# A decoder layer on one core: gate and latent projections as one 144-column matmul, with the latent transposed afterwards

## The chip, the core and the metric

The kernel runs on one core of a Trainium2 chip. The metric is the device time of one execution in microseconds, as the median of several timed runs. Besides these there is one profiled execution, whose trace gives a record for each instruction of each engine: TensorE (PE) for matmuls, with its weight loads listed apart (PEld), VectorE (DVE), ScalarE (ACT), GpSimd (POOL) and SyncE (SP), which issues most of the DMAs. All data are fp32.

## The reference

One decoder layer for 4 batches of 512 tokens with 512 channels. It has three parts, each followed by a residual addition and a layer norm:

- differential causal attention: 8 heads, each from two score maps with a softmax each; their difference weighted by a scalar lambda; a root-mean-square norm of each head's output, and an output projection
- a selective state-space scan over a context input: convolution of 4 taps, projections to step size, B and C, and for 512 channels x 16 states a recurrence over 512 positions; the result is gated by silu of the attention part's output
- a mixture of experts, which is where the change is made. For the tokens x2 of a batch (512 x 512):

```
xl     = x2 @ Wdown.T                        # latent, 512 x 128
probas = sigmoid(x2 @ Wg.T)                  # 16 experts, 512 x 16
w      = the 8 largest of probas + biases keep probas, scaled to a sum of 2.5
acc    = sum_e w[:, e] * ((xl @ rw1[e].T * sqrelu(xl @ rwg[e].T)) @ rw2[e].T)
out    = shared(x2) + acc @ Wup.T
```

Here sqrelu is the squared relu, and shared is a gated unit of the same kind on x2.

## The kernel before

Tokens are tiled by 128 partitions: a batch has four token tiles. Attention runs over 16 units, each a group of two heads and one batch (function attention). The scan (function scan) takes for each batch 16 states x 2 halves of the channels, so 128 steps, each with a product, a recurrence and a second product on DVE, two exponentials on ACT, and an accumulating DMA to a scratch array by POOL. The experts (function experts) run per batch: the scan's result is gated, transposed and added (pt_y), normalized, and the normalized tokens are transposed into x2T (pt_x): four tiles of 128 channels x 512 tokens. From x2T come the routing scores, the latent and the shared part; then follow 16 experts of two halves each (pg, ph, pa), and the output (ps_y).

The routing scores are made with the tokens as weights: for each token tile and each of the four channel tiles, a matmul of 16 columns (w_g), into one PSUM tile ps_gate. Tokens are then on partitions, as the choice of the eight largest needs them: sigmoid on ACT into pr; sc, m8, rp, sp and pr on DVE; then four transposes pt_w, the copy wT, and a DMA to a scratch array, from which each expert's weights are spread over the partitions (wb). The latent is made the other way round, with w_d as weights and x2T as the data: four matmuls of 512 columns into ps_lat, which ACT copies to xl with the latent channels on partitions. That is the layout in which the experts multiply it, as data of pg and, times wb, as data of ph (tile xw).

Nothing is issued in the order of the text. All operations are recorded first with a key, the time at which they are due: nc.key, set by each part of the kernel, plus an offset from the table SHIFT, found by the name of the written tile and the first letter of its engine ("ps_gate.t" is the matmul into ps_gate). The function order then goes through the recorded operations with a fixed table of durations, takes on each engine the ready one with the smallest key, watches how many buffers of a tag are free, and so fixes the order on every engine before the program is built. For this reason all lines of the trace are line 352, where the operations are issued, and groups are told apart by tile names.

Buffers are counted by tag. PSUM: "mm" has three banks (projections, scan inputs, ps_gate, ps_lat, ph, ps_y), "s" three, "tr" one (all transposes), "po" one. In SBUF the tag "c2" has seven slots of 512 columns and holds w_in, w_dt, xm, xd, w_d, yb (batch 0), wb, xw and ht; w_d stays in its slot to the end. w_g takes the slot of w_xp. "pT" has two slots, and w_d and w_g are loaded by one DMA each, on SP's queue, at the key t_unit(15) - 10.

Of the kernel before, what the change touches and what calls it, by code (L numbers as in the profile page):

```python
# [13 lines left out]
AF = mybir.ActivationFunctionType  # L14
# [5 lines left out]
P = 128  # L20
ENGINES = ("tensor", "vector", "scalar", "gpsimd", "sync")

SHIFT = {
    "aT.s": 14, "a_neg.s": 8, "a_neg.v": -9, "bc.s": 7, "bq.s": -2, "cw.s": -2, "da.g": -4, "da.s": -1, "db.s": 3,
    "dt.v": -12, "du.v": 20, "e.s": 8, "e.v": -1, "gb.s": -1, "h.v": -4, "ht.v": -6, "kT.s": 4, "ln_mv.v": -13,
    "ln_nb.v": -7, "ln_rs.g": -2, "ln_st.v": 9, "ln_ve.v": 1, "lo.v": 9, "ls.v": -5, "lt.s": 6, "m.v": -4, "ms.v":
    -4, "nlam.v": -11, "o.s": -17, "obb.s": 9, "pT.s": -3, "pa.t": 1, "pg.t": -4, "pg_s.t": -8, "ph.t": 3,
    "ph_s.t": 3, "po.t": -10, "pr.s": -8, "pr.v": -20, "ps_gate.t": -17, "ps_in.t": -2, "ps_out.t": 5, "ps_v.t":
    1, "ps_x.t": 11, "ps_y.t": -3, "pt_o.t": 3, "pt_w.t": -8, "pt_x.t": 4, "pt_y.t": -12, "relu.s": 23,
    "relu_s.s": -4, "res.g": -4, "res.s": 7, "res.v": -2, "rp.v": -16, "rs.g": 6, "rs.v": -12, "sc.v": -2, "sg.s":  # L30
    -5, "sg.v": 4, "sgc.s": 5, "sh.v": 6, "sp.v": 14, "sq.s": 4, "sub.v": -9, "v.v": 2, "w.s": 7, "wT.s": -1,
    "w_d.s": 4, "w_dt.s": 9, "w_e.s": 24, "w_g.s": 4, "w_in.s": -31, "w_u.s": 1, "w_xp.s": 3, "x2T.s": -13,
    "xd.s": 9, "xl.s": 3, "xm.g": 2, "xm.s": 1, "xw.v": 2, "y.g": -5, "y.s": 6, "y.v": -5, "yb.s": 6, "yb.v": 5,
}
B, S, HID = 4, 512, 512
NT = S // P
# [3 lines left out]
CTX, DI, NST, DTR, KC = 256, 512, 16, 16, 4  # L40
ND = DI // P
LAT, FH, NE, SCALE = 128, 256, 16, 2.5
NEG = -1e30

# [319 lines left out]
def decoder_kernel(  # L366
# [11 lines left out]
    sb = Pool(ctx.enter_context(tc.tile_pool(name="sb", bufs=1)))  # L378
    ps = Pool(ctx.enter_context(tc.tile_pool(name="ps", bufs=1, space=PSUM)), psum=True)
    dram = Pool(ctx.enter_context(tc.tile_pool(name="scratch", bufs=1, space=DRAM)))  # L380

    ident = fixed.tile([P, P], F32, tag="ident", name="ident")
# [10 lines left out]
    nc = Notes(real)  # L393

    def load(shape, src, tag, name=None, bufs=1, most=0):
        t = sb.tile(shape, tag, name or tag, bufs, most)
        nc.sync.dma_start(out=t, in_=src)
        return t

    def small(shape, tag, bufs=8):  # L400
        return sb.tile(shape, tag, tag, bufs)
# [48 lines left out]
    bq = load([P, 32], bqkv, "bq")  # L450
    cw = load([P, ND, KC], convw, "cw")
    cb = load([P, ND], convb, "cb")
    w_in, cT0 = [], sb.tile([P, 2, S], "h", "cT", 5)
    for c in range(2):
        w_in.append(load([P, DI], inT[c * P : (c + 1) * P, :], "c2", "w_in", 7))
        nc.sync.dma_start(out=cT0[:, c, :], in_=ctxT[0, c * P : (c + 1) * P, :])
    xT0 = sb.tile([P, 4, S], "t8", "xT")
    wk0 = load_k(0)
# [4 lines left out]
    w_xp = load([P, ND, 48], xpT.rearrange("(c p) n -> p c n", p=P), "w_xp")  # L463
    lt = load([P, 2, 2, HD], lam4.partition_broadcast(P).rearrange("p (a c d) -> p a c d", a=2, c=2), "qT", "lt", 2)
    sub = load([P, 2], subln, "sub")
    w_dt = load([DTR, DI], dtT, "c2", "w_dt", 7)
    db = load([P, ND], dtb, "db")
    dsk = load([P, ND], dskip, "dsk")
    a_neg = load([P, ND, NST], alog, "a_neg")
# [4 lines left out]
    lp = sb.tile([P, 2, HD], "o", "lp", 2)  # L474
    ls = sb.tile([P, 2], "ls")
    nlam = sb.tile([P, 1], "nlam")
# [8 lines left out]
    res = [sb.tile([P, NT, HID], f"res{b}") for b in range(B)]  # L485
    obb = load([P, HID], ob.partition_broadcast(P), "oT", "obb", 2)
# [10 lines left out]
    y_d = [dram.tile([P, ND, S], f"y{b}") for b in range(B)]  # L497
# [143 lines left out]
    def scan(b):  # L641
# [3 lines left out]
        cT = cT0 if b == 0 else load_cT(b)  # L645
        nc.key = t_scan(b) - (CONV + (AHEAD if b == B - 1 else 0.0)) if b else 0.0
        y = [sb.tile([P, 2, S], "h", "y", 5) for _ in range(2)]
        for d in range(ND):
            pi = ps.tile([P, S], "mm", "ps_in", 3)
            for c in range(2):  # L650
                nc.tensor.matmul(
                    pi, lhsT=w_in[c][:, d * P : (d + 1) * P], rhs=cT[:, c, :], start=(c == 0), stop=(c == 1)
                )
            xm = sb.tile([P, S + KC - 1], "c2", "xm", 7, 2)
            nc.gpsimd.memset(xm[:, : KC - 1], 0.0)
            nc.scalar.copy(xm[:, KC - 1 :], pi)
            cv = y[d // 2][:, d % 2, :]
            nc.scalar.activation(cv, xm[:, :S], AF.Identity, bias=cb[:, d : d + 1], scale=cw[:, d, 0:1])
            for k in range(1, KC):
                nc.vector.scalar_tensor_tensor(cv, xm[:, k : k + S], cw[:, d, k : k + 1], cv, ALU.mult, ALU.add)  # L660
        px = ps.tile([P, S], "mm", "ps_x", 3)
        for k in range(2):
            sg = sb.tile([P, 2, S], "h", "sgc", 5)
            nc.scalar.activation(sg, y[k], AF.Sigmoid)
            nc.vector.tensor_tensor(y[k], y[k], sg, ALU.mult)
        for d in range(ND):
            nc.tensor.matmul(
                px[:48, :], lhsT=w_xp[:, d, :], rhs=y[d // 2][:, d % 2, :], start=(d == 0), stop=(d == ND - 1)
            )
        xd = sb.tile([48, S], "c2", "xd", 7)  # L670
        nc.scalar.copy(xd, px[:48, :])
        nc.sync.dma_start(out=bc_d[b].rows(), in_=xd[DTR:48, :])

# [3 lines left out]
        for k in range(2):  # L677
            dt = sb.tile([P, 2, S], f"dt{k}", "dt")
            du = sb.tile([P, 2, S], f"du{k}", "du")
            lo = sb.tile([P, 2, S], "h", "lo", 5)  # L680
            for j in range(2):
                d = 2 * k + j
# [11 lines left out]
            for j in range(2):  # L694
                d = 2 * k + j
# [4 lines left out]
        for n in range(NST):  # L700
            nc.key = t_scan(b, n) - 15.0
            bc = sb.tile([P, 2, S], "pair", "bc", 2)
            nc.sync.dma_start(out=bc, in_=bc_d[b].state(n))
            for k in range(2):
                nc.key = t_scan(b, n + 0.5 * k)
                h = sb.tile([P, 2, S], "h", "h", 5)
                nc.vector.tensor_tensor(h, dus[k], bc[:, 0:1, :].spread([P, 2, S]), ALU.mult)
                da = das[turn % 2]
                turn += 1
                for j, first in ((0, 0), (1, 1)):  # L710
                    d = 2 * k + j
# [9 lines left out]


    nc.key = t_unit(NG * B - 1) - 10.0
    w_g = load([P, 4, NE], wgT.rearrange("(c p) n -> p c n", p=P), "w_xp", "w_g")
    gb = load([P, NE], gbias.partition_broadcast(P), "gb")
    w_d = load([P, 4, LAT], wdT.rearrange("(c p) n -> p c n", p=P), "c2", "w_d", 7, 1)
    w_s = sb.tile([P, 2, 4, FH], "t8", "w_s")
    nc.sync.dma_start(out=w_s[:, 0, :, :], in_=swgT.rearrange("(c p) n -> p c n", p=P))
    nc.sync.dma_start(out=w_s[:, 1, :, :], in_=sw1T.rearrange("(c p) n -> p c n", p=P))
# [1 line left out]
    w_u = load([P, HID], wuT, "wq", "w_u", 2)  # L731
# [6 lines left out]
    def experts(b):  # L738
        T = t_expert(b)
        nc.key = T - LEAD[b]  # L740
        if b:
            yb = [load([P, 2, S], y_d[b][:, k : k + 2, :], "o", "yb", 2) for k in (0, 2)]
            yb = [yb[d // 2][:, d % 2, :] for d in range(ND)]
        else:
            yb = [load([P, S], y_d[b][:, d, :], "c2", "yb", 7, 4) for d in range(ND)]
        nc.key = max(T - LEAD[b] + 10.0, nc.key + 5.0)
        for i in range(NT):
            sg = sb.tile([P, HID], "pT", "sg", 2)
# [16 lines left out]


        nc.key += 10.0
        pl = ps.tile([P, S], "mm", "ps_gate", 3)
        for i in range(NT):
            for c in range(4):  # L770
                nc.tensor.matmul(
                    pl[:, i * NE : (i + 1) * NE], lhsT=x2T[c][:, i * P : (i + 1) * P], rhs=w_g[:, c, :],
                    start=(c == 0), stop=(c == 3),
                )
        pr = small([P, NT, NE], "pr", 1)
        nc.scalar.activation(pr.flat(), pl[:, : NT * NE], AF.Sigmoid)
        sc = small([P, NT, NE], "sc", 1)
        nc.vector.tensor_tensor(sc, pr, gb.repeat(1, [P, NT, NE]), ALU.add)
        m8 = small([P, NT, 8], "m8", 1)
# [17 lines left out]
        nc.sync.dma_start(out=w_dr[b], in_=wT)  # L797


        pa = ps.tile([P, S], "mm", "ps_lat", 3)  # L800
        for c in range(4):
            nc.tensor.matmul(pa, lhsT=w_d[:, c, :], rhs=x2T[c], start=(c == 0), stop=(c == 3))
        xl = sb.tile([P, S], "kT", "xl", 2)
        nc.scalar.copy(xl, pa)
        nc.key += 5.0
        sh = sb.tile([P, 2, S], "v", "sh", 2)
        for k in range(2):
# [14 lines left out]
        for e in range(NE):  # L822
            nc.key = t_expert(b, e) - WEIGHTS
            w_e = sb.tile([P, 3, FH], "w_e", "w_e", 4)
            nc.sync.dma_start(out=w_e[:, 0, :], in_=rwgT[:, e, :])
            nc.sync.dma_start(out=w_e[:, 1, :], in_=rw1T[:, e, :])
            nc.sync.dma_start(out=w_e[:, 2, :].split(2), in_=rw2T[:, e, :, :])
            wb = sb.tile([P, S], "c2", "wb", 7, 2)
            nc.sync.dma_start(out=wb, in_=w_dr[b].row(e))
            nc.key = t_expert(b, e) - SCALED  # L830
            xw = sb.tile([P, S], "c2", "xw", 7, 2)
            nc.vector.tensor_tensor(xw, xl, wb, ALU.mult)
            for k in range(2):
                nc.key = t_expert(b, e + 0.5 * k)
                pg = ps.tile([P, S], "s", "pg", 3)
                nc.tensor.matmul(pg, lhsT=w_e[:, 0, k * P : (k + 1) * P], rhs=xl, start=True, stop=True)
                ph = ps.tile([P, S], "mm", "ph", 3)
                nc.tensor.matmul(ph, lhsT=w_e[:, 1, k * P : (k + 1) * P], rhs=xw, start=True, stop=True)
                ht = sb.tile([P, S], "c2", "ht", 7, 2)
                glu(pg, ph, ht, sb.tile([P, S], "e", "relu", 3, 2))  # L840
                nc.key += DOWN
                nc.tensor.matmul(
                    pa, lhsT=w_e[:, 2, k * LAT : (k + 1) * LAT], rhs=ht,
                    start=(e == 0 and k == 0), stop=(e == NE - 1 and k == 1),
                )
# [84 lines left out]
```

## Time and profile before

| | |
|---|---|
| timed runs, median of 3 | 1563.35 us (1561.77 to 1566.78) |
| the profiled execution's own time | 1571.12 us |
| its span, first to last instruction | 1569.4 us |
| mean granted TensorE clock | 0.991 |
| PE busy | 1548.7 us, 99% |
| DVE, ACT, POOL busy | 1197.0, 956.5, 196.3 us |
| DMA | 196.18 MB, mean 125 GB/s |

A line of a group reads: line, engine, operation, written tile <- read tiles, shape, count | busy us, mean ns of one | idle time of the engine just before them, and what ended it. A line of the timeline reads: start, length, engine, operation, tiles, number of instructions merged. A line of the stretches gives, for a stretch of time, its length and the busy time of PE, PEld, DVE, ACT and POOL with counts, then the granted PE clock, the DMA engines' busy share and GB/s. Each fp32 matmul makes two records on PE (and two weight loads), a transpose one. The length of a matmul in the trace includes its latency, and the next may start before it ends.

### The profile page before, as it was taken

What the parts mean: (1) busy time and instruction counts of PE and PEld (TensorE: products, weight loads), DVE (VectorE), ACT (ScalarE), POOL (GpSimd) and SP (SyncE); (2) the same over time, 40 slices, a digit from 0 to 9 for tenths busy, and PEclk for the clock granted to TensorE, in tenths of its full rate; (3) what the DMA queues carried; (4) which work ended last, traced back from release to release, by engine and by line L of the source; (5) the groups of instructions that cost most, each with busy time, mean ns of one, the idle gap of its engine ahead of it and who ended that gap; (6) DMA issues with size and microseconds to landing.
All of it is one profiled execution on the core that took longest, in us unless ns stands there. A gap on an engine that the chain in (4) does not pass through costs nothing.

```text
span 1569.4 us, 15790 instructions
## 1 busy us (share of the span) xinstructions
PE 1548.7 (99%) x4944; PEld 851.2 (54%) x4944; DVE 1197.0 (76%) x2036; ACT 956.5 (61%) x2088; POOL 196.3 (13%) x208
## 2 busy tenths in 40 slices
PE   8999999999999999999999999999999999999998
PEld 3566565655656655565665656655445445445443
DVE  6569889687998888898998899898999852542433
ACT  3676566576766557676566668776955553444343
POOL 4101111011111120111111111111111100000000
PEclk9999999998999999999999999999999999999999
DMA  7135576434467663647665566644857741432341
GB/s 264 55 81 108 126 175 141 100 76 99 98 131 190 111 156 61 132 98 152 161 124 126 94 117 155 154 103 101 219 143 151 199 126 54 149 121 76 97 124 51
DMA packets 105523, 196.18 MB, mean 125 GB/s; under 512 B 10896, under 2 KB 45712, under 8 KB 105440
## 3 DMA queue, kind: packets, MB, share of 16 engines
q1 hardware_dynamic: 87008, 128.06, 28.5%
q0 software_dynamic: 18432, 67.12, 25.2%
q8 instruction: 39, 0.64, 0.2%
q14 instruction: 44, 0.36, 0.1%
HBM read 119.25 MB, written 75.89 MB: 124 GB/s over the span
## 4 chain that ended last, share of the span: by engine, by line
PE 96%; DVE 2%; DMA 1%; ACT 1%; issue 1%; SPq 0%; POOLq 0%; DVEq 0%
PE ps_qk L352 21%; PE ps_out L352 14%; PE s L352 9%; PE po L352 9%; PE ps_v L352 7%; PE pa L352 7%; PE pg L352 6%; PE ph L352 6%; PE ps_y L352 3%; PE pt L352 2%; PE pg_s L352 2%; PE ps_in L352 2%; PE ph_s L352 2%; PE pt_o L352 2%; PE ps_dt L352 1%; PE ps_lat L352 1%
## 5 line engine op out<-in xcount | busy, mean ns | idle before, releaser
L352 DVE TENSOR_TENSOR_SCAN h<-da,h 128x1024 f32<-128x1024 f32 x128 | 292.7, 2287 | 2.8
L352 PE MATMUL ps_qk<-xT,wq 128*128 128x512 f32 x512 | 240.5, 593 | 0.0
L352 PE MATMUL ps_out<-ow,oT 128*128 128x512 f32 x512 | 237.6, 595 | 0.0
L352 POOL DMA_DIRECT2D y<-h x128 | 111.3, 869 | 838.2 <-DVE h L352 659.9
L352 ACT ACTIVATE da<-dt,a_neg 128x512 f32<-128x512 f32 (+1 forms) x256 | 174.8, 715 | 45.3 <-DVE h L352 43.6
L352 DVE TENSOR_TENSOR ht<-relu,ph 128x512 f32<-128x512 f32 x128 | 87.2, 684 | 128.8 <-PE ph L352 108.8
L352 PE MATMUL s<-kT,qT 128*128 128x384 f32 (+3 forms) x512 | 170.2, 442 | 0.7 <-DVE nm L352 0.6
L352 PE MATMUL po<-v,pT 128*128 128x256 f32 x640 | 162.1, 384 | 0.4 <-ACT pT L352 0.4
L352 DVE TENSOR_TENSOR h<-h,bc 128x1024 f32<-128x1024 f32 x128 | 156.1, 1219 | 0.9
L352 PEld LDWEIGHTS po<-v,pT 128*128 128x128 f32 x640 | 122.2, 192 | 63.4 <-issue 35.0
L352 DVE TENSOR_TENSOR h<-du,bc 128x1024 f32<-128x1024 f32 x128 | 155.9, 1218 | 0.1
L352 ACT ACTIVATE relu<-pg 128x512 f32<-128x512 f32 x128 | 75.6, 591 | 130.3 <-PE pg L352 116.1
L352 ACT ACTIVATE e<-e,nm 128x128 f32<-128x128 f32 (+3 forms) x256 | 141.8, 556 | 21.6 <-DVE nm L352 20.8
L352 DVE CUSTOM_DVE_ANT_0 e<-s,mask 128x128 f32<-128x128 f32 (+3 forms) x256 | 118.7, 485 | 45.6 <-PE s L352 42.9
L352 PEld LDWEIGHTS ps_out<-ow,oT 128*128 128x128 f32 x512 | 93.3, 191 | 83.1 <-issue 79.8
L352 PEld LDWEIGHTS ps_qk<-xT,wq 128*128 128x128 f32 x512 | 91.9, 190 | 77.3 <-issue 71.9
L352 PE MATMUL pa<-ht,w_e 128*128 128x512 f32 x256 | 131.3, 595 | 1.5 <-DVE ht L352 1.3
L352 PE MATMUL ph<-xw,w_e 128*128 128x512 f32 x256 | 130.3, 592 | 0.0
L352 PE MATMUL pg<-xl,w_e 128*128 128x512 f32 x256 | 129.4, 593 | 0.1
L352 PEld LDWEIGHTS s<-kT,qT 128*128 128x128 f32 x512 | 90.2, 193 | 62.8 <-issue 47.6
L352 PE MATMUL ps_qk<-xT,wk 128*128 128x512 f32 x256 | 120.5, 593 | 0.0
L352 ACT COPY pT<-pt 128x128 f32<-128x128 f32 (+3 forms) x128 | 54.2, 423 | 107.6 <-PE pt L352 106.1
(120 smaller groups left out, 2095.0 us busy)
## 6 DMA issues: line engine op xcount, KB each, us to landing
y<-h POOLq DMA_DIRECT2D x128, 512.0 KB, 7.5
bc<-bc SPq DMA_DIRECT2D x64, 512.0 KB, 6.4
wb<-w SPq DMA_DIRECT2D x64, 256.0 KB, 3.4
xT<-in_xT_dram SPq DMA_DIRECT2D x15, 1024.0 KB, 8.0
w_e<-in_rwgT_dram SPq DMA_DIRECT2D x64, 128.0 KB, 2.2
w_e<-in_rw1T_dram SPq DMA_DIRECT2D x64, 128.0 KB, 2.3
w_e<-in_rw2T_dram SPq DMA_DIRECT2D x64, 128.0 KB, 2.5
wq<-in_wqkvT_dram SPq DMA_DIRECT2D x8, 512.0 KB, 7.2
```

Source lines behind the costliest of these rows:

```text
L352: getattr(getattr(self.nc, s.engine), s.name)(*[get(a) for a in s.args], **{k: get(v) for k, v in s.kw.items()})
```

## The change

The weights w_g (16 columns) and w_d (128 columns) are put side by side in one tile w_dg of 144 columns, with a buffer of its own, filled by two DMAs. For each token tile and channel tile there is one matmul, with the tokens as weights and the 144 columns as data. Two token tiles share a PSUM bank, so ps_gate now consists of two "mm" tiles of 2 x 256 columns, of which 2 x 144 are used. ACT takes the sigmoid of the last 16 columns from each tile, and copies the first 128 columns of each to xr, the latent with tokens on partitions. Four transposes into pt_l (tag "tr") and a copy give xl as before. The matmuls into ps_lat, and w_d and w_g, are gone. The count of "c2" slots becomes C2 = 6, and the whole table SHIFT has new values, so the order of all engines is made anew.

```diff
 SHIFT = {
-    "aT.s": 14, "a_neg.s": 8, "a_neg.v": -9, "bc.s": 7, "bq.s": -2, "cw.s": -2, "da.g": -4, "da.s": -1, "db.s": 3,
...
+    "aT.s": 15.4, "a_neg.s": 12.1, "a_neg.v": -7.8, "bc.s": 7.4, "bq.s": -3.3, "bvb.s": -2.6, "cT.s": -3.5,
...
+    3.2, "po.t": -7.2, "pr.s": -9.5, "pr.v": -13, "ps_dt.t": -0.1, "ps_gate.t": -18.9, "ps_in.t": -1.8,
...
 }
+C2 = 6
...
-        w_in.append(load([P, DI], inT[c * P : (c + 1) * P, :], "c2", "w_in", 7))
+        w_in.append(load([P, DI], inT[c * P : (c + 1) * P, :], "c2", "w_in", C2))
...
-    w_g = load([P, 4, NE], wgT.rearrange("(c p) n -> p c n", p=P), "w_xp", "w_g")
+    w_dg = sb.tile([P, 4, LAT + NE], "w_dg")
+    nc.sync.dma_start(out=w_dg[:, :, :LAT], in_=wdT.rearrange("(c p) n -> p c n", p=P))
+    nc.sync.dma_start(out=w_dg[:, :, LAT:], in_=wgT.rearrange("(c p) n -> p c n", p=P))
     gb = load([P, NE], gbias.partition_broadcast(P), "gb")
-    w_d = load([P, 4, LAT], wdT.rearrange("(c p) n -> p c n", p=P), "c2", "w_d", 7, 1)
...
-        pl = ps.tile([P, S], "mm", "ps_gate", 3)
+        pls, xr = [], sb.tile([P, NT, LAT], "pT", "xr", 2)
+        for k in range(2):
+            pl = ps.tile([P, 2, 256], "mm", "ps_gate", 3)
+            for i in range(2):
+                t = 2 * k + i
+                for c in range(4):
+                    nc.tensor.matmul(
+                        pl[:, i, : LAT + NE], lhsT=x2T[c][:, t * P : (t + 1) * P], rhs=w_dg[:, c, :],
+                        start=(c == 0), stop=(c == 3),
+                    )
+            pls.append(pl)
+        pr = small([P, NT, NE], "pr", 1)
+        for k in range(2):
+            nc.scalar.activation(pr[:, 2 * k : 2 * k + 2, :], pls[k][:, :, LAT : LAT + NE], AF.Sigmoid)
+        for k in range(2):
+            nc.scalar.copy(xr[:, 2 * k : 2 * k + 2, :], pls[k][:, :, :LAT])
+        pt = ps.tile([P, S], "tr", "pt_l", 1)
         for i in range(NT):
-            for c in range(4):
-                nc.tensor.matmul(
-                    pl[:, i * NE : (i + 1) * NE], lhsT=x2T[c][:, i * P : (i + 1) * P], rhs=w_g[:, c, :],
-                    start=(c == 0), stop=(c == 3),
-                )
-        pr = small([P, NT, NE], "pr", 1)
-        nc.scalar.activation(pr.flat(), pl[:, : NT * NE], AF.Sigmoid)
+            nc.tensor.transpose(pt[:, i * P : (i + 1) * P], xr[:, i, :], ident)
+        xl = sb.tile([P, S], "kT", "xl", 2)
+        nc.scalar.copy(xl, pt)
...
-        pa = ps.tile([P, S], "mm", "ps_lat", 3)
-        for c in range(4):
-            nc.tensor.matmul(pa, lhsT=w_d[:, c, :], rhs=x2T[c], start=(c == 0), stop=(c == 3))
-        xl = sb.tile([P, S], "kT", "xl", 2)
-        nc.scalar.copy(xl, pa)
```

More of the change, by code (lines that the diff above doesn't have):

```diff
@@ L23 @@
 SHIFT = {
-    "aT.s": 14, "a_neg.s": 8, "a_neg.v": -9, "bc.s": 7, "bq.s": -2, "cw.s": -2, "da.g": -4, "da.s": -1, "db.s": 3,
[L25 to L33, printed above, removed]
+    "aT.s": 15.4, "a_neg.s": 12.1, "a_neg.v": -7.8, "bc.s": 7.4, "bq.s": -3.3, "bvb.s": -2.6, "cT.s": -3.5,
@@ new lines @@
+    "cf.v": -1.7, "cw.s": -2.2, "da.g": -4.8, "da.s": -1, "db.s": 4.2, "dsk.s": 2.1, "dt.s": -2.1, "dt.v": -7.7,
+    "du.v": 21.2, "e.s": 7.6, "e.v": -2.1, "gb.s": -1.2, "h.v": -4.3, "ht.v": -6.5, "kT.s": 3.9, "l.v": 2.1,
+    "ln_mv.v": -14.5, "ln_nb.v": -33.8, "ln_rs.g": -2.5, "ln_st.v": 4.7, "ln_ve.v": -21.4, "lo.v": 12.6, "lp.v":
+    2.2, "ls.s": -1.8, "ls.v": -6.6, "lt.s": 3, "m.v": -3.7, "ms.v": -4.3, "nlam.v": -8.1, "o.s": -12.8, "oT.s":
+    0.7, "obb.s": 17, "ow.s": -1.2, "pT.s": -2.7, "pa.t": 1, "pg.t": -2.1, "pg_s.t": -8.4, "ph.t": 2.8, "ph_s.t":
@@ new lines @@
+    3.2, "po.t": -7.2, "pr.s": -9.5, "pr.v": -13, "ps_dt.t": -0.1, "ps_gate.t": -18.9, "ps_in.t": -1.8,
+    "ps_out.t": 5.1, "ps_qk.t": 1.3, "ps_v.t": 2.1, "ps_x.t": 12.8, "ps_y.t": 2.9, "pt.t": -0.3, "pt_o.t": 2.7,
+    "pt_w.t": -7.1, "pt_x.t": 1.5, "pt_y.t": -5.9, "qT.s": 0.6, "relu.s": 20.5, "relu_s.s": -3.8, "res.g": -0.4,
+    "res.s": -5.4, "res.v": -1.8, "rp.v": -16.4, "rs.g": 6.5, "rs.v": -12.2, "s.t": 0.9, "sc.v": 4, "sg.s": -1.5,
+    "sg.v": 4.3, "sgc.s": 3.9, "sh.v": 7.5, "sp.v": 15.5, "sq.s": -16.2, "sub.s": -33.5, "sub.v": -9.9, "v.v":
@@ L34 @@
+    1.5, "w.s": 6.4, "wT.s": -1.1, "w_dg.s": 0.9, "w_dt.s": 6.5, "w_e.s": 23.5, "w_in.s": -30.8, "w_s.s": -0.3,
+    "w_u.s": -4.7, "w_xp.s": 1.8, "wb.s": 10.2, "wq.s": 2.4, "wv.s": 5.9, "x2T.s": -13.1, "xd.s": 17.9, "xl.s":
+    2.9, "xm.g": 1.7, "xm.s": 7.8, "xr.s": -1, "xw.v": 3.9, "y.g": -4.6, "y.s": 7.9, "y.v": -9.9, "yb.s": 5.6,
+    "yb.v": 2.7,
 }
@@ L465, in decoder_kernel @@
     sub = load([P, 2], subln, "sub")
-    w_dt = load([DTR, DI], dtT, "c2", "w_dt", 7)
+    w_dt = load([DTR, DI], dtT, "c2", "w_dt", C2)
     db = load([P, ND], dtb, "db")
@@ L653, in scan @@
                 )
-            xm = sb.tile([P, S + KC - 1], "c2", "xm", 7, 2)
+            xm = sb.tile([P, S + KC - 1], "c2", "xm", C2, 2)
             nc.gpsimd.memset(xm[:, : KC - 1], 0.0)
@@ L669, in scan @@
             )
-        xd = sb.tile([48, S], "c2", "xd", 7)
+        xd = sb.tile([48, S], "c2", "xd", C2)
         nc.scalar.copy(xd, px[:48, :])
@@ L744, in experts @@
         else:
-            yb = [load([P, S], y_d[b][:, d, :], "c2", "yb", 7, 4) for d in range(ND)]
+            yb = [load([P, S], y_d[b][:, d, :], "c2", "yb", C2, 4) for d in range(ND)]
         nc.key = max(T - LEAD[b] + 10.0, nc.key + 5.0)
@@ L827, in experts @@
             nc.sync.dma_start(out=w_e[:, 2, :].split(2), in_=rw2T[:, e, :, :])
-            wb = sb.tile([P, S], "c2", "wb", 7, 2)
+            wb = sb.tile([P, S], "c2", "wb", C2, 2)
             nc.sync.dma_start(out=wb, in_=w_dr[b].row(e))
             nc.key = t_expert(b, e) - SCALED
-            xw = sb.tile([P, S], "c2", "xw", 7, 2)
+            xw = sb.tile([P, S], "c2", "xw", C2, 2)
             nc.vector.tensor_tensor(xw, xl, wb, ALU.mult)
@@ L838, in experts @@
                 nc.tensor.matmul(ph, lhsT=w_e[:, 1, k * P : (k + 1) * P], rhs=xw, start=True, stop=True)
-                ht = sb.tile([P, S], "c2", "ht", 7, 2)
+                ht = sb.tile([P, S], "c2", "ht", C2, 2)
                 glu(pg, ph, ht, sb.tile([P, S], "e", "relu", 3, 2))
```

## The prediction, made before the result was known

> **What bounds the kernel now.** I read four views in this order: the page's busy times, the list of what TensorE (PE) waited for, the groups by tile shape, and the timeline of PE around the edited code. The page first.
>
> ```profile
> span 1569.4 us, 15790 instructions
> PE 1548.7 (99%) x4944; PEld 851.2 (54%) x4944; DVE 1197.0 (76%) x2036; ACT 956.5 (61%) x2088; POOL 196.3 (13%) x208
> ```
>
> PE is busy for 1548.7 of 1569.4 us. The 20.7 us that remain are 6.3 at the start, about 7 after its last matmul (it ends at 1562.4) and about 7 of waits in between; the longest waits are these.
>
> ```profile
> PE ps_in L352 <- DMA cT<-in_ctxT_dram: 6.3, 1, 6.3
> PE pt_y L352 <- DVE res L352: 2.4, 3, 0.9
> PE pa L352 <- DVE ht L352: 1.3, 2, 0.8
> ```
>
> (Columns: total us, times, longest.) So what PE has to issue is the time, and an edit is worth what it takes off PE, unless it makes PE wait. The two groups that go, and the transposes that resemble the added ones:
>
> ```profile
> L352 PE MATMUL ps_gate<-w_g,x2T 128*128 128x16 f32 x128 | 15.4, 253 | 0.0
> L352 PE MATMUL ps_lat<-x2T,w_d 128*128 128x512 f32 x32 | 14.5, 592 | 0.0
> L352 PE MATMUL pt_x<-ident,res 128*128 128x128 f32 x64 | 10.3, 279 | 0.2 <-ACT oT L352 0.2
> ```
>
> Each fp32 matmul of the program appears twice here (64 gate matmuls, x128), a transpose once. The means of 253 to 592 ns are latencies that overlap; what counts is the pitch, the distance between starts in a run. It comes from the timeline (start, length, instructions in the run):
>
> ```profile
> 34.43 7.07 PE L352 MATMUL ps_v<-wv,xT 128*128 128x256 f32 x32
> ...
> 41.33 0.61 PE L352 MATMUL s<-kT,qT 128*128 128x128 f32 x4
> ...
> 1049.35 0.60 PE L352 MATMUL pt_x<-ident,res 128*128 128x128 f32 x4
> ...
> 1056.39 2.97 PE L352 MATMUL ps_gate<-w_g,x2T 128*128 128x16 f32 x26
> 1059.21 6.24 PE L352 MATMUL pg_s<-x2T,w_s 128*128 128x512 f32 x10
> ...
> 1192.64 3.60 PE L352 MATMUL ps_lat<-x2T,w_d 128*128 128x512 f32 x8
> ```
>
> Taking off the last one's own latency: 16 columns (2.97 - 0.26)/25 = 0.108 us; 128 columns (0.61 - 0.28)/3 = 0.110; 256 columns (7.07 - 0.38)/31 = 0.216; 512 columns (3.60 - 0.59)/7 = 0.430; transposes (0.60 - 0.27)/3 = 0.110. From 128 columns up the pitch is 0.84 ns a column. At 16 columns it stays at 0.108 us although a seventh of that would stream the data: there the load of 128 weight columns sets it. Between, loading hides behind streaming, as the 128-column run shows.
>
> **PE work, removed and added.** Removed: 128 gate passes x 0.108 = 13.8 us, and 32 latent passes x 0.430 = 13.8 us. Added: 64 matmuls = 128 passes of 144 columns, and 16 transposes pt_l. No row has 144 columns. The lower bound is the load alone, 0.108; the upper is load and stream one after the other, 0.108 + 0.121 = 0.229. I take 144 x 0.84 = 0.121, since the nearest row (128 columns on 128 weights, 0.110) shows full overlap. So 128 x 0.121 = 15.5, and 16 x 0.110 = 1.8. The sum is 17.3 - 27.6 = -10.3 us (bounds -12.0 and +3.5). In the instruction lists of the two built programs every other matmul occurs as often as before, so no other PE work changes.
>
> **The clock around the gate matmuls.** [...] PE's records show stretches at half the granted clock:
>
> ```profile
> 1060.00:1061.00 1.00, 1.00 (x2) 0.41 (x2) 0.97 (x3) 0.17 (x1) 0.00 (x0) 0.50 1.05 211
> ...
> 1432.00:1433.00 1.00, 1.00 (x3) 0.48 (x3) 0.62 (x5) 0.22 (x1) 0.00 (x0) 0.50 0.00 0
> ```
>
> (The last columns are granted clock, DMA share and GB/s.) Both follow a run of 26 gate passes of 16 columns, for batches 0 and 3. Ten passes of pg_s then take 6.24 us where 9 x 0.43 + 0.59 = 4.46 would do, so 1.8 is lost; in batch 3 six take 4.45 for 2.74, 1.7 lost. Batches 1 and 2 have the same matmuls and lose nothing. [...] By the rows, the four pt_w transposes of the same length per batch stand among 512-column matmuls and no half-clock stretch follows them where batches 1 and 2 have them; pt_l stands in the same way, between pg_s, pa and ph_s. I go by the rows: 0 for pt_l, -2 in all, bounds -3.5 and +6.8.
>
> **What ScalarE (ACT), VectorE (DVE) and DMA get.** ACT evicts each gate tile by 2 copies of 256 elements; the row "o<-po 128x256" has 371 ns, so 8 x 0.37 = 3.0 us, and 4 more sigmoids at 0.224 are 0.9. The xl copy stays, from pt_l instead of ps_lat (586 ns). In the built lists ACT loads its tables 38 times and not 42, 4 x 1.28 = -5.1 us. ACT is idle for some 610 us, so none of it shows; without that cover the balance would still be about -1. What can show is latency: pt_l waits for the copies. In batch 0 four pg_s (8 x 0.43 = 3.4 us) lie between the last gate pass and pt_l; the copies, both sigmoids and one table load need at most 0.37 + 1.28 + 0.45 + 0.37 = 2.5. In batch 3 it is two pg_s, 1.7 us, against 0.22 + 0.37 and a handoff of 0.2, with no table load between. In batch 1 the first two pt_l need only the first copy. If one came late, ph_s and the expert matmuls behind pt_l on PE would wait with it, at most about 1 us a batch. DVE's routing chain is unchanged: 2.9 us from sc to pr, against 6.4 us of PE work before pt_w in batch 0. The two weight DMAs remain two; they land in 8.8 and 8.6 us, more than 100 us before use, and keep their place on SyncE's queue just ahead of yb. POOL's queue gets nothing. Pool c2 goes from 7 to 6 slots, but w_d, which held one to the end, no longer lives there; before it was loaded, w_in (2), w_dt, xm (2) and xd make six. Two "mm" banks of three are held during the gate stage, as ps_gate and ps_lat held them in batch 0. All these: 0.
>
> **The new order.** The table of offsets is rewritten, so every engine's order changes, everywhere. At the start, sub goes ahead of w_in and bq, cw and cb behind cT: cT's second half is issued at slot 5 and not 7, some 0.9 us earlier by the pitch of 0.46 us between issues. Then the second ps_x, which waited 0.56 us for y, is reached earlier and can wait for up to 2 us; DVE's y there took 5.1 us for a normal 1.2, while POOL ran the res additions. I take 0, bounds -0.9 and +2. Between 40 and 1034 us PE shows no wait, so a new order can't gain there and can lose; after that about 6 us of waits might go either way. I take +1, bounds -4 and +15.
>
> **Sum.** -10.3 - 2 + 0 + 1 = -11.3 us. The profiled execution took 1571.1 us (its span of 1569.4 and 1.7 around it), so it would take 1559.8. That execution is 7.8 above the median of the timed runs; the same difference on 1563.35 gives 1552.0.
>
> **Rivals.** (1) *Loads not hidden.* If the 144-column pass cost 0.229, the change would be +3.5 on PE, and with -2 and +1 about 1565.9: no change. The 128- and 256-column rows speak against it. (2) *Part of the gain is taken back by DVE.* DVE is busy for 111.65 of the 120 us from 1080 to 1200, where batch 1's gate lies, and 0.9 in the stage before it; if batches 0 and 1 gave nothing, half of 10.3 is left, and with a clock gain of 1 about 1557 to 1560. Against it: PE is full in those same windows, and DVE's remaining tenth is room. (3) *The other side: a worse order in the scan stage.* DVE feeds 128 scan steps (2.29 + 1.22 + 1.22 us each) and the softmax that PE waits for; if the new order blocks s or po behind a scan, PE stands. To end at over 1568 (+4.7) it must lose 4.7 + 12.3 = 17 us, or 0.13 us a scan step; a loss of 20 would give 1571. For it: DVE at 0.9 leaves little room. Against: the work per engine there is the same, and before the change PE had always something ready in this stage.
>
> **How the numbers follow.** A difference under 0.3% (4.7 us) can't be told from none here. The forecast has 0.70 (own range 1544 to 1558), a larger gain through the clock 0.06, rivals 1 and 2 together 0.12, rival 3 0.12. Faster: 0.70 + 0.06 and the 0.02 of rival 2 that ends under 1558.7, 0.78; same 0.10; slower 0.12. Reaching from the largest clock gain (1552 - 9) to the edge of rival 3 leaves out about 2 in 10: 1543 to 1567.
>
> **What would show it.** A ps_gate group of 128x144 x128 with a pitch near 0.12 us (a run of 20 in about 2.6), pt_l x16 near 0.11, PE busy near 1538, no half-clock stretch right after the gate runs, PE waits of 6 to 9 us beyond the start. The prediction is wrong if that pitch is near 0.23, or if waits for DVE between 100 and 1180 us sum to over 10.

## The result, and the profile after

| | before | after |
|---|---|---|
| median of 22 runs each | 1564.67 us | 1557.8 us |
| lowest to highest | 1558.94 to 1570.46 | 1550.21 to 1563.74 |
| ratio, 95% interval | | 0.9958 (0.9944 to 0.9973) |
| span of the profiled execution | 1569.4 us | 1557.0 us |

The change makes the kernel 0.42% faster, about 6.6 us by the ratio. The forecast was 11.3 us, with 1552.0 as the time. So the direction holds and 4 to 5 us are missing. The profiled executions differ by 12.4 us, but single executions of either kernel spread over more than 11 us, so two of them can't be compared to a microsecond. What happened between is seen in the lines.

The page's busy times of the changed kernel:

```profile
span 1557.0 us, 15843 instructions
PE 1534.4 (99%) x4928; PEld 846.0 (54%) x4928; DVE 1204.0 (77%) x2036; ACT 953.2 (61%) x2096; POOL 193.9 (12%) x208
```

PE is still busy for all but 22.6 us, of which 5.9 are the first wait for cT and some 7 the end. Its groups by shape, for the edited code:

```profile
L358 PE MATMUL pg_s<-x2T,w_s 128*128 128x512 f32 x64 | 29.9, 593 | 0.0
...
L358 PE MATMUL ps_gate<-w_dg,x2T 128*128 128x144 f32 x128 | 18.3, 286 | 0.0
...
L358 PE MATMUL pt_l<-ident,xr 128*128 128x128 f32 x16 | 2.6, 273 | 0.0
```

And the timeline around batch 0's gate:

```profile
1062.97 2.61 PE L358 MATMUL ps_gate<-w_dg,x2T 128*128 128x144 f32 x20
1065.42 3.60 PE L358 MATMUL pg_s<-x2T,w_s 128*128 128x512 f32 x8
1068.85 0.60 PE L358 MATMUL pt_l<-ident,xr 128*128 128x128 f32 x4
```

The pitch of a 144-column pass is (2.61 - 0.29)/19 = 0.122 us, against the forecast's 0.121: the weight load hides. The eight pg_s passes behind the run take 3.60 us, which is 7 x 0.43 + 0.59, so at full clock; the group pg_s falls from a mean of 655 ns to 593. pt_l waits for nothing. At the start, though, the list of PE's waits has a new second line:

```profile
PE ps_in L358 <- DMA cT<-in_ctxT_dram: 5.9, 1, 5.9
PE ps_x L358 <- DVE y L358: 5.3, 1, 5.3
PE s L358 <- DVE nm L358: 1.1, 2, 0.6
```

The second ps_x, which waited 0.56 us before, now waits 5.3 for y. The timelines of POOL, DVE and PE tell why. Before:

```profile
23.47 0.42 DVE L352 TENSOR_TENSOR lp<-lt 128x256 f32<-128x256 f32 x1
23.92 0.42 DVE L352 TENSOR_REDUCE ls<-lp 128x2 f32<-128x256 f32 x1
24.70 5.14 DVE L352 TENSOR_TENSOR y<-y,sgc 128x1024 f32<-128x1024 f32 x1 [0.36 <-ACT sgc L352]
...
24.26 18.91 POOL L352 TENSOR_TENSOR res<-res,obb 128x2048 f32<-128x2048 f32 x4 [21.95 <-DMA res<-in_x_dram]
```

After:

```profile
22.30 4.76 DVE L358 TENSOR_TENSOR lp<-lt 128x256 f32<-128x256 f32 x1
27.10 0.42 DVE L358 TENSOR_REDUCE ls<-lp 128x2 f32<-128x256 f32 x1
27.43 5.07 DVE L358 TENSOR_TENSOR y<-y,sgc 128x1024 f32<-128x1024 f32 x1
...
22.26 19.07 POOL L358 TENSOR_TENSOR res<-res,obb 128x2048 f32<-128x2048 f32 x4 [7.49 <-DMA obb<-in_ob_dram]
...
32.55 3.65 PE L358 MATMUL ps_x<-y,w_xp 128*48 128x512 f32 x4 [5.25 <-DVE y L358]
36.13 4.21 PE L358 MATMUL ps_qk<-xT,wq 128*128 128x512 f32 x8
40.17 7.07 PE L358 MATMUL ps_v<-wv,xT 128*128 128x256 f32 x32
```

In the new order SyncE issues res at 13.25 us and not at 17.64, and obb at 14.29 and not at 17.18, so POOL's first addition starts at 22.26 us and not at 24.26. It is then 0.04 us ahead of lp on DVE, which takes 4.76 us for a normal 0.42, until the addition ends; ls behind it takes its normal 0.42 while POOL is at the next addition, and y takes 5.07 us for a normal 1.22. PE stands, and then runs at half clock: the third column from the end of these stretches is the granted clock, 0.50.

```profile
31.00:32.00 1.00, 0.00 (x0) 0.00 (x0) 1.00 (x1) 0.00 (x0) 1.00 (x2) 0.50 0.70 258
36.00:37.00 1.00, 1.00 (x2) 0.50 (x2) 0.97 (x3) 0.58 (x1) 1.00 (x2) 0.50 0.00 0
376.00:377.00 1.00, 1.00 (x2) 0.50 (x2) 1.00 (x3) 0.82 (x2) 0.00 (x0) 0.50 0.61 223
660.00:661.00 1.00, 1.00 (x5) 1.00 (x6) 0.00 (x0) 1.00 (x2) 0.80 (x1) 0.50 0.16 51
```

The first ps_v starts at 40.17 us instead of 34.43: the start costs 5.7 us more than before. From there to the end the changed kernel needs 1557.0 - 40.2 = 1516.8 us, against 1535.0: 18.2 us less in these two executions. Part of that is clock: from there to PE's last matmul the half-clock stretches take 11.9 us from the kernel before and 6.8 from the changed one. The changed kernel's two later stretches, near 376 and 660 us, and those of the kernel before at 56 to 60 and 370 to 381 us all follow the same thing, ps_dt. They are the second reason why neither the spans nor the runs are steady.

In all twelve profiles each half-clock stretch that begins before PE's last matmul lasts 3.4, 6.8 or 10.2 us, so that full work in it loses 1.7 us or a multiple.

### The profile page after: what moved, and what is told of

It reads as the page before. It is cut to its first block, busy times and chain, and to the rows that moved or that the text cites. A ratio compares the mean times of both kernels' runs of the same rounds, so it can differ in the third digit from the quotient of the medians.

```text
span 1557.0 us, 15843 instructions
## 1 busy us (share of the span) xinstructions
PE 1534.4 (99%) x4928; PEld 846.0 (54%) x4928; DVE 1204.0 (77%) x2036; ACT 953.2 (61%) x2096; POOL 193.9 (12%) x208
## 4 chain that ended last, share of the span: by engine, by line
PE 96%; DVE 3%; ACT 0%; DMA 0%; issue 0%; SPq 0%; POOLq 0%; ACTq 0%
PE ps_qk L358 21%; PE ps_out L358 14%; PE s L358 9%; PE po L358 9%; PE ps_v L358 7%; PE pa L358 7%; PE ph L358 7%; PE pg L358 7%; PE ps_y L358 3%; PE pt L358 2%; PE pg_s L358 2%; PE ph_s L358 2%; PE pt_o L358 2%; PE ps_in L358 2%; PE ps_dt L358 1%; PE ps_gate L358 1%
## 5 line engine op out<-in xcount | busy, mean ns | idle before, releaser
L358 ACT ACTIVATE sq<-po 128x256 f32<-128x256 f32 x128 | 48.7, 381 | 115.4 <-PE po L358 114.6
```

The source lines that it names most:

```text
L358: getattr(getattr(self.nc, s.engine), s.name)(*[get(a) for a in s.args], **{k: get(v) for k, v in s.kw.items()})
```

## The experiments

The time of a run, multiplied by the mean granted clock of that run, gives about what it would take at full clock; the rest is lost to half-clock stretches. These two columns are rough: the clock is given in steps of 0.001, which is 1.6 us, and in every profile the clock is half behind PE's last matmul too, which counts 0.6 to 2.4 us as lost that cost nothing. Each kernel was run beside the kernel before on the same chip. Medians, in us:

| kernel | median (runs) | range | ratio to before | at full clock | lost to the clock |
|---|---|---|---|---|---|
| before, beside the experiments (45) | 1564.2 | 1558.6 to 1574.2 | | 1555.5 | 9.4 |
| changed | 1557.8 (22) | 1550.2 to 1563.7 | 0.9958 | 1547.4 | 10.9 |
| e1: edit, old table | 1552.3 (6) | 1548.8 to 1555.5 | 0.9921 (0.9894 to 0.9948) | 1545.6 | 7.0 |
| e2: new table alone | 1572.0 (12) | 1565.7 to 1577.7 | 1.0051 (1.0031 to 1.0070) | 1559.9 | 13.4 |
| e3: changed, POOL split | 1552.1 (6) | 1548.2 to 1556.7 | 0.9922 (0.9892 to 0.9952) | 1542.7 | 9.3 |
| e9: before, ps_dt on 96 rows | 1556.5 (10) | 1554.6 to 1559.7 | 0.9940 (0.9919 to 0.9961) | 1550.0 | 6.2 |
| e10: e1 with 96 rows | 1540.7 (6) | 1540.5 to 1542.8 | 0.9844 (0.9813 to 0.9875) | 1539.0 | 1.5 |
| e11: e2 with 96 rows | 1562.5 (12) | 1552.0 to 1566.8 | 0.9967 (0.9941 to 0.9993) | 1553.7 | 7.8 |
| e12: changed with 96 rows | 1548.5 (6) | 1539.7 to 1551.9 | 0.9888 (0.9854 to 0.9921) | 1543.8 | 4.6 |
| e8: changed, split, 96 rows | 1539.6 (6) | 1539.3 to 1540.2 | 0.9841 (0.9815 to 0.9867) | 1538.0 | 1.5 |
| e13: e10 with the split | 1542.2 (4) | 1540.6 to 1544.1 | 0.9854 (0.9818 to 0.9890) | 1539.6 | 1.5 |
| e14: e8 once more | 1538.8 (4) | 1538.8 to 1540.2 | 0.9835 (0.9806 to 0.9864) | 1537.2 | 1.5 |

### The edit and the table apart

The change has two parts that have nothing to do with each other: the matmuls, and a new table of offsets. e1 makes the edit with the old table; up to batch 0's gate its instructions stand on every engine as in the kernel before, but for the two weight DMAs.

```diff
 # the changed kernel, with the values of SHIFT of the kernel before
-    "w_d.s": 4, "w_dt.s": 9, "w_e.s": 24, "w_g.s": 4, "w_in.s": -31,
+    "w_dg.s": 4, "w_dt.s": 9, "w_e.s": 24, "w_in.s": -31,
```

> The edit with the old table of offsets: every engine has the order of the kernel before up to batch 0's gate. My theory: the edit is worth 10.3 us of PE (gate pitch 0.12 us) and up to 3.5 of half clock behind the gate runs, and the start is as before (second ps_x waits about 0.6 us, first ps_v near 34.4 us), so 10 to 14 us faster than before. Rival, DVE takes part of the edit's gain back in the scan stage: about 7 us faster, the same as the changed kernel, with new PE waits for DVE after 1050 us.

Measured: 1552.3 us, 0.79% or 12.3 us faster. The start is the old one: ps_x waits 0.8 us and the first ps_v begins at 34.03. Of new waits for DVE after 1050 us there are two of 0.3 us (ph for xw, pt for e). The gate's lines are those of the changed kernel:

```profile
1051.14 2.61 PE L353 MATMUL ps_gate<-w_dg,x2T 128*128 128x144 f32 x20
1053.59 4.45 PE L353 MATMUL pg_s<-x2T,w_s 128*128 128x512 f32 x10
```

Ten pg_s in 4.45 us, where the kernel before took 6.24 behind its 16-column run. So the edit gives what the sum of the forecast said, and DVE took back 0.6 us at most. What was missing came from the table.

e2 has the old matmuls and the new table.

```diff
 # the kernel before, with the values of SHIFT of the changed kernel
-    1.5, "w.s": 6.4, "wT.s": -1.1, "w_dg.s": 0.9, "w_dt.s": 6.5,
+    1.5, "w.s": 6.4, "wT.s": -1.1, "w_d.s": 0.9, "w_g.s": 0.9, "w_dt.s": 6.5,
```

> The old gate and latent matmuls with the new table (w_d and w_g take w_dg's offset): the start has the order of the changed kernel. My theory: the second ps_x waits about 5 us for DVE's y, the first ps_v starts near 40 us and not 34.4, and the kernel is 3 to 7 us slower than before. Rival, the table costs nothing: within 2 us of before, and what the changed kernel lacks against the forecast was lost at the gate.

Measured: 1572.0 us, 0.51% slower, some 8 us. The table does cost time, and more than expected, but in the profiled execution not in the way expected: there ps_x waited only 1.1 us.

```profile
22.66 0.42 DVE L357 TENSOR_TENSOR lp<-lt 128x256 f32<-128x256 f32 x1
23.11 0.42 DVE L357 TENSOR_REDUCE ls<-lp 128x2 f32<-128x256 f32 x1
23.86 4.83 DVE L357 TENSOR_TENSOR y<-y,sgc 128x1024 f32<-128x1024 f32 x1 [0.34 <-ACT sgc L357]
...
23.09 18.91 POOL L357 TENSOR_TENSOR res<-res,obb 128x2048 f32<-128x2048 f32 x4 [20.78 <-DMA obb<-in_ob_dram]
```

Here lp was done 0.01 us before POOL began. So whether the start costs 1 us or 5 is a race between two engines that start within tenths of a microsecond of each other. This execution is no longer than the profiled one of before (1569.3 and 1569.4 us), so it doesn't show the 8 us. Both lose to the clock before PE's last matmul, before 11.9 us and e2 13.7: in e2 half-clock stretches stand at 368 to 379, 654 to 659 and 927 to 935 us, each beginning at a group of ps_dt, and at 1197 to 1201 and 1313 to 1317 behind 16-column gate runs.

### The race at the start

e3 keeps all orders of the changed kernel and issues each of POOL's four long additions as four short ones.

```diff
+            if s.engine == "gpsimd" and s.name == "tensor_tensor" and columns(s.args[0]) == NT * HID:
+                r, obb = s.args[0], s.args[2].buf.view
+                for i in range(NT):
+                    self.nc.gpsimd.tensor_tensor(get(r[:, i, :]), get(r[:, i, :]), get(obb), s.args[3])
+                continue
             getattr(getattr(self.nc, s.engine), s.name)(
```

> The changed kernel, each of POOL's four additions of ob to res (128x2048) issued as four of 128x512, all orders kept. My theory: DVE instructions were held until the POOL instruction that ran beside them ended; with short ones lp, y and nlam of the start take at most 2.5 us and not 4.4 to 5.1, the wait of ps_x falls from 5.3 to under 1.5 us, the first ps_v starts before 36 us, and the kernel gains 4 to 7 us on the changed one, 11 to 14 on before. Rival, DVE waits there for data or DMA traffic: lp and y stay at 4.5 to 5 us, no gain.

Measured: 1552.1 us, 5.7 below the changed kernel. lp and y are no longer held to the end of a long addition, ps_x waits for nothing, and the first ps_v begins at 33.43 us.

```profile
23.12 1.50 DVE L363 TENSOR_TENSOR lp<-lt 128x256 f32<-128x256 f32 x1
24.66 0.42 DVE L363 TENSOR_REDUCE ls<-lp 128x2 f32<-128x256 f32 x1
24.99 1.84 DVE L363 TENSOR_TENSOR y<-y,sgc 128x1024 f32<-128x1024 f32 x1
...
22.55 21.31 POOL L361 TENSOR_TENSOR res<-res,obb 128x512 f32<-128x512 f32 x16 [6.96 <-DMA obb<-in_ob_dram]
```

lp again starts behind POOL's first (by 0.57 us; 0.04 in the changed kernel) and takes 1.50 us, not 4.76; y takes 1.84. So it was the length of POOL's instruction that held DVE, not data. Beside the long additions of the changed kernel lp took 4.76 us, y 5.07, nlam 4.45 and a_neg 4.40; ls beside them, and v beside those of the kernel before, took 0.42. What sets the held instructions apart was not tried.

### The clock at ps_dt

The profile of e3 had four half-clock stretches before PE's last matmul, each beginning at a group of ps_dt or within 1 us behind it. These multiply 16 rows of xd by w_dt: inside a group PE streams 512 columns at the usual pitch of 0.43 us, but on 16 rows (16*128 in the listing) where the other groups have 128. e8 pads w_dt, and w_xp before it, with zeros to 96, so the same matmuls use 96 rows.

```diff
-    w_xp = load([P, ND, 48], xpT.rearrange("(c p) n -> p c n", p=P), "w_xp")
+    w_xp = sb.tile([P, ND, 96], "w_xp")
+    nc.gpsimd.memset(w_xp, 0.0)
+    nc.sync.dma_start(out=w_xp[:, :, :48], in_=xpT.rearrange("(c p) n -> p c n", p=P))
...
-    w_dt = load([DTR, DI], dtT, "c2", "w_dt", C2)
+    w_dt = sb.tile([96, DI], "c2", "w_dt", C2)
+    nc.gpsimd.memset(w_dt, 0.0)
+    nc.sync.dma_start(out=w_dt[:DTR, :], in_=dtT)
...
-                px[:48, :], lhsT=w_xp[:, d, :], rhs=y[d // 2][:, d % 2, :], start=(d == 0), stop=(d == ND - 1)
+                px[:96, :], lhsT=w_xp[:, d, :], rhs=y[d // 2][:, d % 2, :], start=(d == 0), stop=(d == ND - 1)
...
-        xd = sb.tile([48, S], "c2", "xd", C2)
-        nc.scalar.copy(xd, px[:48, :])
+        xd = sb.tile([96, S], "c2", "xd", C2)
+        nc.scalar.copy(xd, px[:96, :])
...
-                nc.tensor.matmul(pd, lhsT=w_dt[:, d * P : (d + 1) * P], rhs=xd[:DTR, :], start=True, stop=True)
+                nc.tensor.matmul(pd, lhsT=w_dt[:, d * P : (d + 1) * P], rhs=xd, start=True, stop=True)
```

> The kernel with the split additions, and the weights of ps_dt (16 rows) and the columns of w_xp padded with zeros to 96, so that ps_dt works on 96 rows; orders kept, same results, no more PE time by the pitch. Theory: half-clock stretches near 375 and 658 us follow the ps_dt matmuls because these use 16 of 128 rows; with 96 none follow them, ps_dt's mean falls from 683 to about 600 ns, and the time is 2 to 6 us below that of the split alone. Rival, the stretches come from the transposes and short runs around ps_dt, or from chance: they stay, and the time is within 2 us of the split alone.

Measured: 1539.6 us, 12.5 below e3 and twice what was expected, and the runs lie within 1 us of one another where e3's lie within 8.5. ps_dt's mean is 592 ns. The same stages in both, e3 first:

```profile
371.00:372.00 1.00, 1.00 (x4) 0.57 (x3) 0.92 (x3) 0.49 (x2) 0.00 (x0) 0.50 0.49 174
654.00:655.00 1.00, 1.00 (x2) 0.00 (x0) 0.61 (x1) 0.01 (x1) 0.09 (x1) 0.50 0.11 21
```

and e8, which comes to these stages 5 and 10 us earlier, and where no stretch up to PE's last matmul is at half clock:

```profile
366.00:367.00 1.00, 1.00 (x3) 0.38 (x2) 1.00 (x3) 1.00 (x3) 0.00 (x0) 1.00 0.90 254
644.00:645.00 1.00, 1.00 (x7) 0.70 (x6) 1.00 (x3) 1.00 (x3) 0.00 (x0) 1.00 0.69 135
```

In the five profiles with 16 rows (before, changed, e1, e2, e3) twelve half-clock stretches begin at ps_dt, in 12 of their 20 batches; in the seven with 96 rows (e8 to e14) none does, in 28. ps_x, which the padding widens too, ends more than 20 us before each of these groups, so it is no rival.

The clock is not all that the padding gave. The same groups at full clock, in e3 and then in e8:

```profile
365.75 1.98 PE L363 MATMUL ps_dt<-xd,w_dt 16*128 16x512 f32 x4
367.66 0.66 PE L363 MATMUL pt_o<-ident,o 128*128 128x128 f32 x4
368.24 1.12 PE L363 MATMUL ps_dt<-xd,w_dt 16*128 16x512 f32 x2
...
361.70 1.88 PE L363 MATMUL ps_dt<-xd,w_dt 96*128 96x512 f32 x4
363.42 0.60 PE L363 MATMUL pt_o<-ident,o 128*128 128x128 f32 x4
363.85 1.02 PE L363 MATMUL ps_dt<-xd,w_dt 96*128 96x512 f32 x2
```

From the start of the first group to that of the second it is 2.49 us and 2.15. Over the whole traces a group of ps_dt on 16 rows costs 0.28 us more than on 96, whether it has 2 passes or 6, and a group of ps_x with 48 columns 0.22 more than with 96: it is the change to another shape and back that costs. With 13 and 7 such groups this is 5.2 us in the changed kernel, and with 11 and 6 it is 4.4 in the order of the old table. So of the 12.5 us some 5 are work at full clock, as the table has it (1542.7 to 1538.0), and some 7 to 8 are clock. Whether the few rows bring the half clock, or the short gaps at the change of shape, is not separated, since padding removes both. How many rows are enough was not tried.

### Edit and table again, without the noise of ps_dt

With 96 rows the runs of a kernel lie within some 5 us or fall into groups, so that the parts can be priced. These are before, e1, e2 and the changed kernel, each with the diff of the last section.

> The kernel before with ps_dt on 96 rows (weights and w_xp padded with zeros; orders kept, same results). Theory: the clock lost at ps_dt goes and that behind the 16-column gate runs stays, so the time falls by 4 to 7 us to 1556 to 1559, half-clock stretches are left only behind gate runs, the transposes near 1038 us and at the end, and the runs still differ by 2 us or more. Rival, gate runs cost no clock either, what stood behind them was chance: no stretch there, runs within 1 us of one another.

Measured: 1556.5 us (e9), 7.7 below the kernel before, of which 4.4 are the changes of shape. It keeps half-clock stretches behind two of its four 16-column gate runs, and has none near 1038 us:

```profile
1041.55 2.97 PE L352 MATMUL ps_gate<-w_g,x2T 128*128 128x16 f32 x26
1044.37 5.80 PE L352 MATMUL pg_s<-x2T,w_s 128*128 128x512 f32 x9
```

The view ends in the ninth pg_s pass; 5.80 us is 1.8 more than the 8 x 0.43 + 0.59 of nine passes at full clock. Its runs still spread over 5 us.

> The edit with the old table, ps_dt on 96 rows. Against the same without the edit (the run before this one) this is the price of the edit with the clock's chance taken out: by the sum of the forecast 10.3 us of PE and 0 to 3.5 us of gate clock, so 10 to 14 us less, about 1545 to 1547. Rival, DVE's load takes part of it back: 5 to 8 us less, with new PE waits for DVE after 1050 us.

Measured: 1540.7 us (e10), so 15.7 below e9: by the table 1550.0 - 1539.0 = 11.0 at full clock, and 6.2 - 1.5 = 4.7 of clock. The two profiles have 3.4 of clock, behind two gate runs, and 10.1 of the rest. By the medians the edit is worth more than the 10 to 14 us expected, by the profiles (13.5) it is not; DVE takes back 0.6 us at most. Over all profiles the four 16-column runs were followed by a half-clock stretch in two batches each time, 8 of 16 (before, e2, e9, e11), and the 144-column runs in none of 32 (changed, e1, e3, e8, e10, e12, e13, e14). The added pt_l transposes stand in all of these 32.

> The old gate and latent matmuls with the new table, ps_dt on 96 rows. Theory: what the new table cost (8 us against before) was mostly clock at ps_dt, so with 96 rows it is within 3 us of the kernel before with 96 rows, unless the second ps_x waits for y at the start (then 4 to 8 us slower). Rival, the new table costs by its order: 6 us or more slower with PE waits spread over the span.

Measured: 1562.5 us (e11), in two groups: five runs from 1552.0 to 1556.7 and seven from 1562.2 to 1566.8. The profiled one is of the second group:

```profile
PE ps_x L357 <- DVE y L357: 5.6, 1, 5.6
```

The slower group is 5.8 to 10.4 us above e9, so the expected 4 to 8 us of the start came there, and partly more; the median of the faster group is 0.9 below e9. By the medians the new table still costs 6 of its 8 us with 96 rows, so the theory that its price was mostly clock at ps_dt does not hold: it lies mostly in the start. That the faster runs won the race is inferred from their times.

> The changed kernel with ps_dt on 96 rows, POOL's additions not split. Against the kernel with both (1539.6 us) this is the price of POOL's long additions at the start: 5 to 8 us if lp meets the first addition as in the changed kernel's profile (1545 to 1548, second ps_x waits about 5 us), or 0 to 2 us in executions where lp comes ahead of it; so either a steady 1545 or runs in two groups. Rival, the split has no part in it: within 1 us of 1539.6 in all runs.

Measured: 1548.5 us (e12): one run at 1539.7, the others from 1547.3 to 1551.9. In the profiled one, at 1546.5 us of span, ps_x waits 5.5 us, to 33.8, and PE is at half clock from 32.4 to 39.2. The run at 1539.7 is where the split is always. So the race costs nothing when it is won. When it is lost it costs some 8 us by this trace, 5.5 of the wait and 2.7 of slow clock behind it, and 8 to 12 by the runs; what the slowest two lost besides has no trace. That the one fast run won the race is inferred from its time.

> The edit with the old table, ps_dt on 96 rows, and POOL's additions split: the version with the three gains together. Theory: the 1 to 2 us that the second ps_x and DVE's held instructions cost at the start go too, 1538 to 1540 us with all runs within 2 us. Rival, the old order has nothing to gain from the split: 1540.5 to 1543 in two groups, as without it.

> The changed kernel with the split additions and ps_dt on 96 rows once more, beside the old table's version on the same chip. Theory: without the two causes of loss the tables differ by less than 2 us, so the price of the new table (8 us) lay wholly in the start and the clock at ps_dt. Rival, the new order costs 3 us or more elsewhere.

Measured: 1542.2 us (e13) and 1538.8 (e14). e13 missed its expectation. The split set DVE free at 24 us, but then "cf" took 4.17 us (0.22 where POOL was done) beside POOL's short additions, and PE waited behind it:

```profile
40.93 4.17 DVE L358 SCALAR_TENSOR_TENSOR cf<-l,nlam,l 128x1 f32<-128x1 f32 x1
...
45.53 0.33 PE L358 MATMUL pt<-ident,e 128*128 128x128 f32 x1 [1.68 <-DVE e L358]
```

cf ended at 45.10 us and POOL's last addition at 45.08. So a row of short POOL instructions doesn't always let DVE in between; in e3 it did at lp and y, in e8 at y. e14, the same program as e8, confirms it. Without the two losses the new order is not worse than the old one but better, by 1.2 us (e8 against e10) to 3.4 (e14 against e13, where 1.7 is the wait behind cf); less than 2 had been expected. So the table's price lay in the start and at ps_dt. e8 is the fastest version found, 1.6% faster than before.

## Why the prediction was right in direction and short in size

**PE work, removed and added.** Right. The sum was -10.3 us; e9 and e10 give -11.0 at full clock by the medians and -10.1 by the profiles. The pitch of 144 columns was 0.122 for 0.121, and pt_l took the 0.110 of other transposes. That at 16 columns the weight load sets the pitch fits the trace: from 1056.5 to 1059.0 us, inside the run, PEld is busy for all 2.50 us. Rival 1, loads not hidden, is out.

**The clock around the gate matmuls.** Right in kind, too small in size: I took -2, with -3.5 and +6.8 as bounds. The -3.5 is what the kernel before lost in its two stretches (1.8 and 1.7); the 2 and the +6.8 are shown by no run. What the runs showed in their place: all four profiles with 16-column runs lose 3.4 behind them, and those with 144 columns nothing, with the four transposes pt_l in each of their 32 batches; by the medians of e9 and e10 it was 4.7, and the 1.3 above the profiles isn't accounted for. The rows by which I took 0 for pt_l were read too narrowly: the kernel before has a half-clock stretch from 1039 to 1043 us too, behind 16 transposes pt_y with 1.6 us of waits among them. e1 has the same transposes and waits and no such stretch, so its cause stays open.

**ACT, DVE, DMA at the gate.** Right: pt_l waited for nothing in the changed kernel, and rival 2, DVE taking part of the gain back, is out by e1 and e10 but for 0.6 us. PE's list of waits after shows none from ps_lat's removal or from C2 = 6.

**The new order.** This is the step that failed. At the start I saw that ps_x would be reached earlier and that POOL's additions held y, and still took 0 with a bound of +2. The term was mis-sized: the wait was 5.3 us in the changed kernel's profile, and with the half-clock stretch behind it the lost race costs 8 to 12 us (e12). The 2 us bound held only y itself to be blocked. It did not ask what else could be: with res loaded earlier POOL starts 2 us sooner, lp is caught first, and y is held by the next addition. Nor did I price half-clock stretches at ps_dt, though the profile had them near 56 and 370 us and I had counted those behind the gate runs; the reading stopped at the edited code. 96 rows gave 7.7 us to the kernel before (1564.2 to 1556.5) and 9.3 to the changed one (1557.8 to 1548.5), which has more groups of ps_dt and ps_x. From the kernel before to the changed one the medians go by these steps: the edit -15.7 (e9 to e10), the new order with the split -1.2 (e10 to e8), the start +8.9 (e8 to e12), and +1.6 for what 96 rows give the one more than the other. The sum is -6.4, as measured; it has to close, since each step starts where the last one ended, so it shows the sizes and not that each step has one cause.

**What was luck.** Two misses cancelled in part: the edit gave 15.7 us where 12.3 were counted (10.3 of PE work and 2 of clock), and the order took 9.3 where 1 was counted. Had the edit given only its 12.3, the time would have lain some 3 us above the forecast's own range of 1544 to 1558, into which it falls by 0.2.

**Rival 3, a worse order.** It had the right sign and the wrong place. The scan stage from 400 to 1040 us has PE busy for 640.00 of 640 us after the change, with 3.4 us lost to half clock near 660. The main loss sat in the first 40 us, where the forecast's price per scan step says nothing.

## What to carry to other kernels

An edit that comes with a new order is two changes: run each alone, because here one gave -12 and the other +8. When PE is full, look not only for what it waits for but for stretches at half clock, and at what PE did just before them: here these were runs of 16 columns (8 of 16 batches) and groups of 16 rows (12 of 20), although PE counted as busy. Padding the few rows with zeros cost nothing here, and even saved PE time, 0.28 us a group of ps_dt. Where POOL and DVE start long instructions within a microsecond of each other, count with the slower outcome of the race, here 8 us and more (e12).

## What was not expected of the hardware

- Groups of matmuls on 16 of 128 rows were followed by PE at half clock in 12 of 20 batches; on 96 rows, with zeros as the added weights, in none of 28. With the changes of shape this was worth 7.7 to 12.5 us of 1560, and the runs of e3, which differ by 8.5 us, differ by 0.9 in e8. PE's records are busy for 1.00 of 1 us at the granted clock of 0.50 in the stretches shown (371 and 654 us of e3, 376 and 660 of the changed kernel), and for 3.00 of the 3 us before each of these four half-clock stretches begins.
- A change from 128 rows to 16 and back costs PE 0.28 us a group, and one from 128 weight columns to 48 and back 0.22; to 96 rows or columns the same traces show nothing of it.
- PE's wait of 5 us at the start came with half clock: PE was at it from 30.4 to 37.2 us in the changed kernel, and had work from 32.55, so 2.3 us were lost besides the wait. e11 and e12, which waited 5.6 and 5.5 us, have such a stretch too, and the nine profiles where ps_x waited 1.1 us or less have none there.
- Starts of two engines that differ by tenths of a microsecond or less (0.04 us in the changed kernel) decide over 8 us and more, and the runs of one program fall into two groups (e11, e12).
